# Moving side work between the hooks of a hand-scheduled macaron block: convolution sums one step ahead of their products, moments and the half chunk spread, a few rescales from VectorE to ScalarE

## Chip, cores and metric

The kernel runs on one core of one Trainium2 chip. The metric is device microseconds of one launch, the median of the runs. The profiled execution is a separate launch: it has a time of its own, and a span from its first to its last instruction in the trace.

## What is computed

The input `u` is 2 x 1024 x 1024 in fp32, that is 2048 rows of 1024. Three residual stages follow each other, the first and the third with the same 4-bit weights:

```python
x = x + 0.5 * ffn(layernorm(x))
x = x + s4(layernorm(x))            # long convolution over the last axis
x = x + 0.5 * ffn(layernorm(x))

def ffn(x):                         # W = scales[group] * (w4 - (z4[group] + 1)), groups of 128 rows
    h = silu(x @ Wg) * (x @ Wu)     # Wg, Wu: 1024 x 2752
    return h @ Wd                   # Wd: 2752 x 1024

def s4(u):                          # K: 1024 taps from 64 complex poles
    y = irfft(rfft(u, n=2L) * rfft(K, n=2L), n=2L)[..., :L]
    return y + D[0] * u
```

The kernel computes the convolution as products with 128 x 128 Toeplitz blocks of K, made from Lambda, p, q, Vc, B, Ct and the step size while other work runs.

## The kernel before

**Jobs.** The 2048 rows are cut into four blocks of 512 (`TB`), each held as four tiles of 128 rows. A job is one block in one of the two feed-forward stages; `JOBS` (L756) lists eight: blocks 0 and 1 in stage 1, blocks 0 and 1 in stage 3, then the same for blocks 2 and 3. They are numbered j = 0 to 7. A job is `gate_up` (L766) followed by `down` (L856). The convolution of a block whose stage-1 job was j-1 runs beside the `gate_up` of job j, so in jobs 1, 2, 5 and 6. The tables of K are made once, beside `gate_up` of job 1.

**gate_up.** 64 steps, numbered s: eight waves (`WAVES`) of eight groups g of 128 input rows. The first five waves hold three chunks of 128 output columns each, the last three two; the very last also has the half chunk, which is the 64 columns left over from 2752. A chunk has two units, gate (even number) and up (odd number). A unit owns one of the eight 512-column PSUM banks. In a step each unit gets two products (L795), one with the low part of the normalized input in fp16 and one with the high part in fp32r. The group scale is not put into the weights. After each group except the last the running sum in PSUM is multiplied by a ratio of scales (`scaled`, L758): a rescale, by ScalarE at L760 (called ACT in the profile) or by VectorE at L764 (DVE). Even units go to ACT, odd ones to DVE, and in jobs 0 and 1 the first odd unit of the wave goes to ACT in some steps (L808). After the last group of a wave, `gated` (L820) makes silu of the gate on ACT (L822), multiplies by the up unit on DVE (L825), and splits the result on GpSimd (POOL) into an fp32r high part (L827) and a low part (L829). `gated_half` (L832) does so for the half chunk; its split (L844, L846) is run on DVE at once in job 0, and on POOL at steps 1 and 2 of `down` in the other jobs.

**down.** 44 steps, numbered d: two halves a of the 1024 output columns, each with 22 chunks f. A step has eight products (L870), on four banks c, and then four rescales: banks 0 and 2 on ACT, 1 and 3 on DVE, and in job 0 bank 1 also on ACT at even f (L878). The results go back to rows and into x at hooks of the next job.

**Weights.** Weight bytes are loaded four steps ahead by SyncE (SP, `load_bytes`, L713) and cast three steps ahead by POOL (`make_weights`, L730, the cast at L737), into five buffers.

**Hooks.** All other work is cut into pieces by generators, and `fast` (L1512) hangs each piece on a step of `up` or `dn`; a half step means the middle of the step. Some pieces are wrapped in `in_order_of_writing` (L143) or `pinned`, which adds order dependencies on the named engines only. Otherwise the order on each engine is settled by a scheduler when the program is built, which takes the order of writing as its starting point but need not keep it. The pieces that the change touches:

- moments (`moments_by_tile`, L182: eight bn_stats of 128x512 and four small aggregates, and then `guess`, L196, three tiny instructions), deviations (`deviations_in_pieces`, L213: three Newton steps of three tiny instructions each, and a factor), normalizations (L259, L263), all on DVE. In job 0 they are for block 1 and hang on `down` of job 0. There `turn_by_pool` (L243) follows: four transposes on PE, a copy on ACT, a cast and a subtraction on POOL, for each half tile.
- in `down` of job 1 the normalizations for job 2 (L1646), and `turn_by_dma` (L265), which splits on POOL and transposes by DMA.
- the tables (`s4_tables`, L1207): 63 pieces spread over steps 1 to 42 of `gate_up` of job 1 (L1618). They hold small products on PE (`s4_sums` L1076, `s4_k` L1156, and two of 128x512 from L1185 on), and many small operations on DVE and POOL.
- the convolution (`convolve`, L1219): six block sums in three instructions on POOL (L1227 to L1229), then products in two halves (L1232), then additions into x on DVE. For tile t it hangs on `gate_up` at a base step o: turning from o on, the store at o+4, the load of columns at o+7, sums and the first half of the products at o+10, the second half at o+11 (L1570 to L1577).

Of the kernel before, what the change touches and what calls it, by code (L numbers as in the profile page):

```python
# [32 lines left out]
GK = 8  # L33
# [24 lines left out]
def macaron_s4_kernel(  # L58
# [123 lines left out]
    def moments_by_tile(b, k, halves=False):  # L182
# [11 lines left out]
        guess(b, k, mv)  # L194

    def guess(b, k, mv):  # L196
        name = f"{b}_{k}"
        ve = small.tile([P, NT], F32, tag="ve", name=f"ve_{name}")
        nc.vector.tensor_scalar(ve, mv[:, :, 1], EPS, None, ALU.add)
        r = small.tile([P, NT], F32, tag="r", name=f"r_{name}")  # L200
        half = small.tile([P, NT], I32, tag="half", name=f"half_{name}")
        nc.vector.tensor_scalar(half, ve.bitcast(I32), 1, None, ALU.logical_shift_right)
        nc.vector.tensor_scalar(
            r.bitcast(I32), half, -1.0, float(0x5F3759DF), ALU.mult, ALU.add
        )
        ln[b] = (mv, ve, r)
# [559 lines left out]
    def gate_up(j, b, hooks):  # L766
        hi, lo = pieces[b]
        ps = {}
        for s, (wi, g) in enumerate(STEPS):
# [9 lines left out]

            early = (len(order) + 1) // 2  # L780
            turns = [(k, pos, k == 1) for k in range(2) for pos in range(early)]
            turns += [(k, pos, k == 0) for k in (1, 0) for pos in range(early, len(order))]
            for i, (k, pos, done) in enumerate(turns):
# [21 lines left out]
                if g < GK - 1:  # L805
                    on_act = unit % 2 == 0
                    if unit == 2 * fs[0] + 1:
                        on_act = (j == 0 and g % 4 == 0) or (j == 1 and g % 2 == 0)  # L808
                    if unit == 2 * WIDE:
                        on_act = g % 2 == 0  # L810
# [21 lines left out]
    def gated_half(j, p):  # L832
# [15 lines left out]
        half_split[j] = split(nc.gpsimd if j else nc.vector)  # L848
        if j == 0:
            for _ in half_split[j]:  # L850
                pass

    half_split = {}
    yT = {}

    def down(j, b, hooks):  # L856

        steps = [(a, f) for a in range(NH) for f in range(NF)]
        for d, (a, f) in enumerate(steps):
# [5 lines left out]
            for c in range(4):  # L865
# [12 lines left out]
                on_act = c % 2 == 0 or (j == 0 and c == 1 and f % 2 == 0)  # L878
                if f < GD - 1:
# [179 lines left out]
    def s4_roots():  # L1059
# [13 lines left out]
        for i in range(2):  # L1073
            src = c_eight[i].rearrange("(r v c) -> r v c", r=8, v=8)[:, 0, :]
            nc.sync.dma_start(eight[:, i], src.partition_broadcast(P))
        ps = bank("s4_sums")  # L1076
# [57 lines left out]
    def s4_response():  # L1134
# [20 lines left out]
        yield  # L1155
        ps = bank("s4_k")  # L1156
# [10 lines left out]
    def s4_toeplitz():  # L1167
# [14 lines left out]
        for i in range(NH):  # L1182
            for _ in range(4 - 2 * i):
# [33 lines left out]
    S4_PIECES = 63  # L1217

    def convolve(b, t, s, name):  # L1219
# [9 lines left out]
        nc.gpsimd.tensor_tensor(sums[:, 3], sums[:, 0], sums[:, 1], ALU.add)  # L1229

# [281 lines left out]
    def fast():  # L1512
# [5 lines left out]
        for j, (b, k) in enumerate(JOBS):  # L1518
# [7 lines left out]
            if prev:  # L1526
# [9 lines left out]
                if pk == 1:  # L1536
                    first, start_, gap = (26, 36, 3.5) if j == 1 else (13, 23, 4)
                    steps = [(up, first + (i if j == 1 else (3 * i // 2) / 2)) for i in range(8)]
                    in_pieces(at, steps, lambda: moments_by_tile(pb, 2, halves=True))
                    steps = [(up, start_ + i - 4 if j != 1 else start_ - 2 + i / 2) for i in range(4)]  # L1540
# [29 lines left out]
                    for t in range(NT):  # L1570
# [4 lines left out]
                        at(up, o + 7, pinned(lambda t=t: columns_loaded(t), ET.SP))  # L1575
                        at(up, o + 10, lambda t=t: conv(t))
                        at(up, o + 11, lambda t=t: next(parts[t], None))  # L1577
                    steps = [(up, start_ + gap * t + 13 + i) for t in range(NT) for i in range(2)]
                    in_pieces(at, steps, lambda: moments_by_tile(pb, 3, halves=True))
                    done = start_ + gap * 3 + 15  # L1580
                    steps = [(up, done + i / (2 if j == 1 else 1)) for i in range(4)]
# [32 lines left out]
            if j == 1:  # L1614
                tables = s4_tables()
                for i in range(S4_PIECES):
                    piece = lambda: in_order_of_writing(lambda: next(tables, None), ET.DVE)
                    at(up, 1 + 42 * i // S4_PIECES, piece)  # L1618
            if j == 3:
                in_pieces(at, [(up, 36 + i) for i in range(24)], in_order)  # L1620
            if after:
                ab, ak = after
                if ak == 1:
                    at(up, 55 if j == 0 else 6, lambda: load_x(ab, rows_of(u, ab)))
                    if j == 0:
                        steps = [(dn, d) for d in range(4, 22, 2)]
                        in_pieces(at, steps, lambda: moments_by_tile(ab, 1, halves=True))
                        steps = [(dn, d) for d in (20.5, 21, 21.5, 22)]
                        in_pieces(at, steps, lambda: deviations_in_pieces(ab, 1, LIFT))
                    else:  # L1630
                        steps = [(up, s) for s in range(12, 21)]
# [12 lines left out]
                for t in range(NT):  # L1644
                    for half in range(2):
                        d, where = (23 + 4 * t + 2 * half if j == 0 else (0.5, 6, 14, 20)[t] + half), dn  # L1646
# [5 lines left out]
                    if j == 0:  # L1652
                        for half in range(2):
                            piece = lambda t=t, half=half: turn_by_pool(ab, t, half)
                            at(dn, 25 + 4 * t + 2 * half, piece)
                        continue
                    late = (12, 13) if t == NT - 1 else (13, 17)
                    for d in (1, 2, 3, 5, 6, 7, 9) + late:
                        piece = lambda t=t: turning(t)
                        piece = lambda piece=piece: in_order_of_writing(piece, ET.Pool, ET.SP)  # L1660
                        at(dn, 2 + 9 * t + d, piece)
            for d in (1, 2) if j else ():
# [225 lines left out]
```

## Time and profile before

| what | value |
|---|---|
| runs | 2067.83, 2064.02, 2063.87 us; median 2064.02 |
| the profiled execution, its time | 2064.28 us |
| its span in the trace | 2062.2 us |
| from the start to the first product of job 0 | 22.6 us |
| `gate_up` of job 0 | 178.3 us, PE busy 166.81 |
| `down` of job 7 ends at | 2051.8 us; 10.4 us follow |
| the costliest rescales | L760 on ACT, pg: 1256 of 660 ns; L764 on DVE, pg: 1152 of 691 ns |

A group in the profile is one line of the program, one engine, one operation and one kind of tile, with busy time, mean duration and the idle time ahead of it. The tile names are those of the program: `pg` is a bank of `gate_up`, `po` one of `down`, `pc` and `pb` are the convolution's, `xTh` and `xTl` the two parts of the input, `hh` and `hl` those of the gated product, `hb` the half chunk. The profiler's names for the engines are PE (TensorE), PEld (its weight loads), DVE (VectorE), ACT (ScalarE), POOL (GpSimd) and SP (SyncE). PEclk is the clock that the chip granted to TensorE, as a share of full speed.

### The profile page before, as it was taken

The numbers are of one execution on the slowest core, as the hardware profiler recorded it, in microseconds if no ns is written. First come the engines' busy times: TensorE is split into PE (matmuls) and PEld (weight loads), VectorE is DVE, ScalarE is ACT, GpSimd is POOL, SyncE is SP. The second block draws the span as 40 slices with busy tenths as digits, with TensorE's granted clock in tenths as the row PEclk, the third lists the DMA queues.
The fourth block names the chain that finished last, engine by engine and source line by source line (L and its number), as shares of the span: only waits on it lengthen the run. The fifth ranks groups of instructions, "written<-read, shape, count | busy, mean of one in ns | idle before, by whom it ended". The sixth has DMA issues, their size and how long they took to land.

```text
span 2062.2 us, 29944 instructions
## 1 busy us (share of the span) xinstructions
PE 2011.6 (98%) x9204; PEld 1370.9 (66%) x9204; DVE 1666.7 (81%) x2861; ACT 1397.5 (68%) x2185; POOL 1349.8 (65%) x1740
## 2 busy tenths in 40 slices
PE   6999999999999999999999999999999999999998
PEld 4555675567866778655876568667686576866576
DVE  8888978777888787888778877887878878777777
ACT  6777787756675476767777777664776646767775
POOL 5867668656875478755867568763696645965542
PEclk9999999999999999999999999999999999999999
DMA  4435323233623327511462116333163331661113
GB/s 139 124 90 146 110 83 84 56 83 89 172 78 80 92 50 166 165 32 35 112 176 94 32 46 159 97 77 85 45 156 109 72 92 41 152 186 46 34 35 102
DMA packets 346888, 197.16 MB, mean 96 GB/s; under 512 B 168069, under 2 KB 324590, under 8 KB 346718
## 3 DMA queue, kind: packets, MB, share of 16 engines
q1 hardware_dynamic: 345414, 192.74, 35.0%
q8 instruction: 75, 1.23, 0.3%
q10 hardware_dynamic: 1016, 1.82, 0.2%
q14 instruction: 95, 0.78, 0.1%
q0 software_dynamic: 288, 0.59, 0.1%
HBM read 127.52 MB, written 48.57 MB: 85 GB/s over the span
## 4 chain that ended last, share of the span: by engine, by line
PE 88%; DVE 4%; POOL 2%; DMA 2%; issue 1%; ACT 1%; SPq 0%; ACTq 0%; POOLq 0%; DVEq 0%
PE pg L795 54%; PE po L870 29%; PE pc L1232 3%; PE pb L1232 1%; DVE pg L764 1%; DMA b<-wq 1%; POOL hh L827 0%; DMA bd<-wdq 0%; POOL hl L829 0%; ACT pg L760 0%; POOL w_up L737 0%; POOL q L644 0%; DVE po L764 0%; ACT g L822 0%; DMA x<-in_L_attn_u_dram 0%
## 5 line engine op out<-in xcount | busy, mean ns | idle before, releaser
L760 ACT ACTIVATE pg<-pg,rat 128x512 f32<-128x512 f32 x1256 | 794.0, 660 | 399.5 <-PE pg L795 396.7
L764 DVE TENSOR_TENSOR pg<-pg,rat 128x512 f32<-128x512 f32 x1152 | 764.7, 691 | 144.7 <-PE pg L795 136.9
L795 PE MATMUL pg<-xTh,w_up 128*128 128x512 f32 x2752 | 854.2, 438 | 2.6 <-DVE pg L764 1.3
L795 PE MATMUL pg<-xTl,w_up 128*128 128x512 f16 x2752 | 718.4, 382 | 10.5 <-DVE pg L764 4.3
L737 POOL CAST w_up<-b 128x768 fp32r<-128x768 int8 (+2 forms) x490 | 374.8, 771 | 399.2 <-PE pg L795 289.1
L795 PEld LDWEIGHTS pg<-xTh,w_up 128*128 128x128 f32 x2752 | 519.2, 189 | 171.2 <-issue 10.3
L760 ACT ACTIVATE po<-po,ratd 128x512 f32<-128x512 f32 x660 | 433.4, 662 | 155.5 <-PE po L870 155.1
L870 PE MATMUL po<-hl,w_down 128*128 128x512 f32 x1344 | 526.2, 394 | 5.7 <-DVE po L764 5.4
L870 PE MATMUL po<-hh,w_down 128*128 128x512 f32 x1344 | 520.6, 390 | 0.0
L764 DVE TENSOR_TENSOR po<-po,ratd 128x512 f32<-128x512 f32 x620 | 429.3, 695 | 110.1 <-PE po L870 109.4
L795 PEld LDWEIGHTS <-w_up 128*128 128x128 bf16 x2752 | 226.5, 98 | 350.2 <-issue 168.5
L737 POOL CAST w_down<-bd 128x512 fp32r<-128x512 int8 x352 | 217.6, 621 | 155.1 <-PE po L870 77.9
L870 PEld LDWEIGHTS po<-hl,w_down 128*128 128x128 f32 x1344 | 251.7, 188 | 69.5 <-DVE po L764 11.3
L870 PEld LDWEIGHTS po<-hh,w_down 128*128 128x128 f32 x1344 | 252.4, 188 | 50.9
L829 POOL TENSOR_TENSOR hl<-hf,hh 128x512 fp32r<-128x512 f32 x168 | 218.7, 1302 | 7.0
L827 POOL CAST hh<-hf 128x512 fp32r<-128x512 f32 x168 | 107.5, 640 | 74.5 <-DVE hf L825 44.2
L825 DVE SCALAR_TENSOR_TENSOR hf<-pg,rat,g 128x512 f32<-128x512 f32 x168 | 122.5, 747 | 37.1 <-ACT g L822 28.8
L822 ACT ACTIVATE g<-pg,rat 128x512 f32<-128x512 f32 x168 | 110.1, 686 | 44.5 <-PE pg L795 29.0
L922 POOL TENSOR_TENSOR x<-x,yr 128x512 f32<-128x512 f32 x52 | 66.7, 1283 | 0.0
L289 POOL TENSOR_TENSOR lo<-x,hi 128x512 f16<-128x512 f32 x48 | 61.8, 1288 | 0.0
L189 DVE BATCH_NORM_STATS2 stats<-x 128x6 f32<-128x512 f32 x88 | 59.9, 680 | 0.0
L287 POOL TENSOR_TENSOR mid<-hi,top 128x512 bf16<-128x512 f32 x48 | 56.0, 1166 | 0.0
(216 smaller groups left out, 1080.2 us busy)
## 6 DMA issues: line engine op xcount, KB each, us to landing
b<-wq SPq DMA_DIRECT2D x319, 96.0 KB
bd<-wdq SPq DMA_DIRECT2D x336, 64.0 KB
x<-in_L_attn_u_dram SPq DMA_DIRECT2D x30, 512.0 KB
yz<-y SPq DMA_DIRECT2D x56, 256.0 KB
yr<-yz SPq DMA_DIRECT2D x56, 256.0 KB
b<-wq SPq DMA_DIRECT2D x128, 64.0 KB
sz<-xn SPq DMA_DIRECT2D x16, 512.0 KB
st<-sz SPq DMA_DIRECT2D x64, 128.0 KB
```

The source lines that it names most:

```text
L289: nc.gpsimd.tensor_tensor(lo[:, own], n[:, own], hi[:, own].bitcast(F32), ALU.subtract)
L737: nc.gpsimd.tensor_copy(t, b)
L760: nc.scalar.activation(dst, src, AF.Copy, scale=sc)
L764: nc.vector.tensor_tensor(dst, src, sc.to_broadcast(list(dst.shape)), ALU.mult)
L795: nc.tensor.matmul(p, weights, (lo, hi)[k][:, g, :], start=(g == 0 and not done), stop=(g == GK - 1 and done), skip_group_check=True,)
L822: nc.scalar.activation(g, pg, AF.Silu, scale=rat[:, 2 * f, GK - 1 :])
L825: nc.vector.scalar_tensor_tensor(hf, pu, last, g, ALU.mult, ALU.mult)
L827: nc.gpsimd.tensor_copy(hi, hf)
L829: nc.gpsimd.tensor_tensor(lo, hf, hi.bitcast(F32), ALU.subtract)
L870: nc.tensor.matmul(ps[c], w[:, bass.ts(c, P)], part, start=(f == 0 and k == 0), stop=(f == NF - 1), skip_group_check=True,)
L922: nc.gpsimd.tensor_tensor(part, part, rows_back.pop((a, t)), ALU.add)
L1232: nc.tensor.matmul(dst, lhsT, rhs, start=start, stop=stop, skip_group_check=True)
```

## The change

It has nine edits. No arithmetic is added or removed; work moves in time or between engines.

- `convolve` yields after its three sums. The sums now hang on o+9, the first half of the products on o+10, the second on o+11; the columns are loaded at o+6 instead of o+7.
- `guess` becomes `guess_in_pieces`, its three instructions in three pieces. So the moments have two pieces more, and every list of their steps is lengthened by two (or one).
- In `gate_up`, in the last group of a wave of three chunks, the fourth and fifth unit change places in PE's order.
- In jobs 3 and 4 the first odd unit of a wave is rescaled by ACT in steps 25 to 32.
- The half chunk of job 0 is split on POOL, at steps 12 and 13 of `down`.
- In `down`, bank 1 is rescaled by ACT in seven steps of job 1 and in three steps of job 7.
- The tables get empty pieces: two ahead of `s4_sums`, two more ahead of `s4_k`, two more ahead of the first large product, and none between the first and the second (two fewer). They run as 69 pieces over 43 steps.
- Beside `gate_up` of the convolving jobs, moments and deviations shift by a step or half a step.
- In `down` of job 0 the moments run at steps 4 to 16 in steps of 1.5 instead of 4 to 20, the deviations at 17 to 20 instead of 20.5 to 22, normalizations and transposes one step later. In `down` of job 1 the first normalizations stand at steps 2 and 3 instead of 0.5 and 1.5, and the first tile's turning one step later.

```diff
-        guess(b, k, mv)
+        yield from guess_in_pieces(b, k, mv)
...
+    def guess_in_pieces(b, k, mv):
...
         nc.vector.tensor_scalar(ve, mv[:, :, 1], EPS, None, ALU.add)
+        yield
...
         nc.vector.tensor_scalar(half, ve.bitcast(I32), 1, None, ALU.logical_shift_right)
+        yield
...
+            if n == 3 and g == GK - 1:
+                order[3], order[4] = order[4], order[3]
...
                         on_act = (j == 0 and g % 4 == 0) or (j == 1 and g % 2 == 0)
+                        on_act = on_act or (j in (3, 4) and 24 < s < 33)
...
-        half_split[j] = split(nc.gpsimd if j else nc.vector)
-        if j == 0:
-            for _ in half_split[j]:
-                pass
+        half_split[j] = split(nc.gpsimd)
...
+    relief = {1: (2, 3, 6, 7, 14, 15, 20), len(JOBS) - 1: (36, 38, 40)}
...
                 on_act = c % 2 == 0 or (j == 0 and c == 1 and f % 2 == 0)
+                on_act = on_act or (c == 1 and d in relief.get(j, ()))
...
+        yield
+        yield
         ps = bank("s4_sums")
...
+        yield
+        yield
         yield
         ps = bank("s4_k")
...
-            for _ in range(4 - 2 * i):
+            for _ in range(6 - 4 * i):
                 yield
...
-    S4_PIECES = 63
+    S4_PIECES = 69
...
         nc.gpsimd.tensor_tensor(sums[:, 3], sums[:, 0], sums[:, 1], ALU.add)
+        yield
...
-                    first, start_, gap = (26, 36, 3.5) if j == 1 else (13, 23, 4)
+                    first, start_, gap = (25, 36, 3.5) if j == 1 else (13, 23, 4)
                     steps = [(up, first + (i if j == 1 else (3 * i // 2) / 2)) for i in range(8)]
+                    steps += [(up, first + 7.5 if j == 1 else 18.5), (up, first + 8 if j == 1 else 19)]
...
-                    steps = [(up, start_ + i - 4 if j != 1 else start_ - 2 + i / 2) for i in range(4)]
+                    steps = [(up, start_ + i - 3.5 if j != 1 else start_ - 2 + i / 2) for i in range(4)]
...
-                        at(up, o + 7, pinned(lambda t=t: columns_loaded(t), ET.SP))
-                        at(up, o + 10, lambda t=t: conv(t))
+                        at(up, o + 6, pinned(lambda t=t: columns_loaded(t), ET.SP))
+                        at(up, o + 9, lambda t=t: conv(t))
+                        at(up, o + 10, lambda t=t: next(parts[t]))
                         at(up, o + 11, lambda t=t: next(parts[t], None))
...
+                    steps += [(up, start_ + gap * 3 + 14.5), (up, start_ + gap * 3 + 15)]
...
-                    steps = [(up, done + i / (2 if j == 1 else 1)) for i in range(4)]
+                    steps = [(up, done + 0.5 + i / (2 if j == 1 else 1)) for i in range(4)]
...
-                    at(up, 1 + 42 * i // S4_PIECES, piece)
+                    at(up, 1 + 43 * i // S4_PIECES, piece)
...
-                        steps = [(dn, d) for d in range(4, 22, 2)]
+                        steps = [(dn, 4 + (3 * i) / 2) for i in range(8)] + [(dn, 15.5), (dn, 16)]
...
-                        steps = [(dn, d) for d in (20.5, 21, 21.5, 22)]
+                        steps = [(dn, d) for d in (17, 18, 19, 20)]
...
-                        steps = [(up, s) for s in range(12, 21)]
+                        steps = [(up, s) for s in range(12, 21)] + [(up, 20.5)]
...
-                        d, where = (23 + 4 * t + 2 * half if j == 0 else (0.5, 6, 14, 20)[t] + half), dn
+                        d, where = (24 + 4 * t + 2 * half if j == 0 else (2, 6, 14, 20)[t] + half), dn
...
-                            at(dn, 25 + 4 * t + 2 * half, piece)
+                            at(dn, 26 + 4 * t + 2 * half, piece)
...
-                        at(dn, 2 + 9 * t + d, piece)
-            for d in (1, 2) if j else ():
+                        at(dn, 2 + 9 * t + d + (j == 1 and t == 0), piece)
+            for d in (1, 2) if j else (12, 13):
```

More of the change, by code (lines that the diff above doesn't have):

```diff
@@ L193, in moments_by_tile @@
             yield
-        guess(b, k, mv)
+        yield from guess_in_pieces(b, k, mv)
     def guess(b, k, mv):
+        for _ in guess_in_pieces(b, k, mv):
+            pass
+    def guess_in_pieces(b, k, mv):
         name = f"{b}_{k}"
```

## The prediction

> **What bounds the kernel now.** I read the page's busy shares first.
>
> ```profile
> span 2062.2 us, 29944 instructions
> ...
> PE 2011.6 (98%) x9204; PEld 1370.9 (66%) x9204; DVE 1666.7 (81%) x2861; ACT 1397.5 (68%) x2185; POOL 1349.8 (65%) x1740
> ```
>
> PE, the matrix engine, is busy 98% of the span, and 88% of the chain that ended last is PE at lines 795 and 870. No product is removed, so only PE's waits can be won. Of its 50.6 us of idleness (2062.2 - 2011.6), 14.7 lie before the first product (22.6 us, of which small work on PE fills 7.86) and 8.4 behind the last (10.4, 2.04 filled); the change touches neither. Another 11.5 (178.3 - 166.81) lie in the up stage of job 0, where only the swapped pair acts. So 16.0 us are within reach. The second view is the busy time in the stretches between the first products of the stages: here down of job 0, up and down of jobs 1 and 2, up of jobs 3, 4 and 7, down of job 7.
>
> ```profile
> core 0: us, PE busy (x) PEld busy (x) DVE busy (x) ACT busy (x) POOL busy (x), PEclk, DMA share, GB/s
> 200.90:292.90 92.00, 87.45 (x394) 67.62 (x392) 74.35 (x129) 69.44 (x113) 66.94 (x96) 1.00 0.34 98
> 292.90:483.30 190.40, 187.83 (x905) 118.62 (x905) 146.65 (x295) 128.83 (x209) 120.65 (x182) 1.00 0.32 82
> 483.30:564.20 80.90, 79.73 (x347) 63.90 (x346) 67.44 (x102) 55.45 (x85) 70.05 (x90) 1.00 0.52 131
> 564.20:747.30 183.10, 181.06 (x880) 116.98 (x880) 152.13 (x282) 110.39 (x174) 100.53 (x123) 1.00 0.29 76
> 747.30:825.70 78.40, 78.40 (x346) 64.50 (x344) 61.15 (x94) 55.52 (x85) 68.82 (x90) 1.00 0.59 136
> 825.70:982.20 156.50, 155.62 (x691) 92.93 (x691) 132.63 (x231) 110.45 (x174) 93.23 (x114) 1.00 0.25 75
> 1060.60:1216.50 155.90, 155.21 (x689) 93.31 (x689) 128.73 (x213) 110.48 (x174) 92.17 (x111) 1.00 0.25 74
> 1817.90:1972.80 154.90, 154.90 (x690) 93.33 (x689) 117.90 (x180) 110.54 (x174) 91.53 (x111) 1.00 0.25 76
> 1972.80:2051.80 79.00, 79.00 (x346) 64.16 (x344) 63.27 (x102) 55.63 (x85) 30.52 (x46) 1.00 0.24 70
> ```
>
> The third figure is the length, and stages with the same products can be compared. An undisturbed down stage takes 78.4, an undisturbed up stage without convolution 154.9. Job 0's down is 13.6 above that; its 48 transposes at some 0.11 us each explain 5.3, so 8.3 are waits and the slack around them. Job 1's down is 2.5 above, job 3's up 1.6, job 4's 1.0, job 7's down 0.6. Job 1's up is 7.3 above job 2's, of which its table products (20 small ones at some 0.11, 4 of 128x512 in fp32 at some 0.4) explain 3.8. The clock is 1.00 in all of them. The third view, PE's waits, names the causes.
>
> ```profile
> PE pb L1232 <- POOL sums L1227: 5.7, 6, 1.7
> PE pg L795 <- DVE pg L764: 5.6, 15, 0.8
> PE po L870 <- DVE po L764: 5.4, 7, 1.8
> ```
>
> Asked by stage: the first row is 1.9 in each of jobs 2, 5 and 6, none in job 1. Of the second, 3.5 lie in job 0's up and 0.7 each in jobs 1, 3 and 4. Of the third, 4.3 lie in job 0's down and 1.2 in job 1's. Job 1's up adds 0.9 (tables, POOL), 0.6 (tables, DVE) and 0.4 (tables, a DMA).
>
> **Sums a step ahead.** This is the headline, worth up to 5.7 us of waits and about 0.4 us per job of restarting PE. The wait is made here, in POOL's timeline:
>
> ```profile
> 655.33 0.61 POOL L827 CAST hh<-hf 128x512 fp32r<-128x512 f32 x1
> 655.90 0.99 POOL L1227 TENSOR_TENSOR sums<-st 128x384 f32<-128x384 f32 x1
> 656.84 1.27 POOL L829 TENSOR_TENSOR hl<-hf,hh 128x512 fp32r<-128x512 f32 x1
> ```
>
> PE's product on the sums starts at 656.94, when the first of them is done. But the order in which the engines execute is not the order of the hooks: a scheduler places each instruction. Comparing both built programs engine by engine, POOL's and SP's orders, and the waits on them, are the same from the middle of job 1's down to the end: in job 2 the sums still stand behind the cast of chunk 11 and ahead of its low part. PE's order there differs only in the swapped pair. So I give this edit nothing in jobs 2, 5 and 6 (bounds 0 to 6.9). In job 1 it moves sums of tiles 1 to 3 by one place and loads for tile 2 ahead of one weight load on SP; PE did not wait there, so 0.
>
> **Job 0's down.** Three things change. First, the half chunk leaves DVE for POOL. DVE's rows of it beside POOL's of the other seven jobs:
>
> ```profile
> L844 POOL CAST hb<-hf_half x7: 609/610/687, 489.5 to 1978.6; 64x512 fp32r<-64x512 f32 x7
> L846 POOL TENSOR_TENSOR hb<-hf_half,hb x7: 1285/1288/1291, 490.2 to 1980.0; 64x512 fp32r<-64x512 f32 x7
> L844 DVE CAST hb<-hf_half x1: 424/424/424, 202.3 to 202.3; 64x512 fp32r<-64x512 f32 x1
> L846 DVE TENSOR_TENSOR hb<-hf_half,hb x1: 1582/1582/1582, 203.5 to 203.5; 64x512 fp32r<-64x512 f32 x1
> ```
>
> On DVE it costs 0.42 + 1.58 + 0.06 of gaps = 2.06 us at 202.3 to 205.1, ahead of the first rescale (205.80), for which PE waits until 206.54, then until 209.91 for the next two. On POOL it costs 0.61 + 1.29 = 1.90 around steps 12 and 13, where POOL is busy 5.9 us of 10 (221 to 231) and the chunk isn't used until step 21: hidden. The Trainium skill speaks against such a move: its page "Perfetto Trace Analysis", section "Optimizing Scalar/DVE Operations", warns that the two engines share a port to SBUF, so that offloading from one to the other might not help. By the rule the gain would be near 0. The row for it: in job 3 a normalization took 1.47 instead of 0.53 us at 913.76, while POOL's 1.29 us subtraction (913.66 to 914.95) ran. By the rows, though, that price is paid once, at most 1.3 us, at a step where DVE is not waited for, while the 2.06 go where PE stands still. I take the rows: the second rescale follows its product instead of DVE's queue, 1.8 us (bounds 0.7 to 2.1).
>
> Second, eight moments of about 0.6 us start in steps 4 to 14.5 instead of 4 to 20, and the 14 tiny instructions of guess and deviations (0.5 us each at 243.85 to 246.7, then 0.16) go from steps 20 to 22 into steps 15.5 to 20. Today they hold up the last rescales of the first half, and PE waits 1.8 us until 250.90. Third, normalizations and transposes stand one step later. Summing DVE's durations between successive rescales in the new order gives 32.5 us for 17 steps of 1.83 = 31.1, with a lag of up to 2 us in steps 15 to 20; DVE is busy 9.7 of 10 us at 231 to 241 already. So of 1.8 + 0.2 us waited there now, and 0.3 of restarting, I keep 1.0 as a new wait nearer the middle: 1.3 us won (bounds 0 to 2.6). Together **3.1 us**.
>
> **Job 1's up.** Table pieces run 69 in 43 steps instead of 63 in 42, so each is some 6% earlier until the added empty steps before three products. In the new order DVE's last pole weights stand before the three gated chunks instead of between them, POOL's response sums before cast 35 instead of behind chunk 10, and the two turning products at steps 38 and 39 instead of 36 and 38. The waits 0.6, 0.9 and 0.4 and their restarts (2.3 in all) should go. What becomes late is POOL's building of the tables: 5.9 us that now stand behind chunks 12 to 14. Counted through with POOL's durations, cast 46 ends at 420.7 on the old clock, against step 46 at 421.3: 0.6 us of cover, and where it fails PE waits the difference, up to 1.5 us. ScalarE's copy of the first half (0.7) now stands ahead of three gates. I subtract 0.6 for both: **1.7 us** (bounds 0 to 3).
>
> **Rescales to ScalarE.** Job 1's down, steps 2, 3, 6, 7, 14, 15, 20: exactly where normalizations stand; tile 0's move to 2 and 3. PE's 1.2 us of waits with restarts are 1.7, and 0.8 more is slow pitch around them; ScalarE then has three rescales of 0.60 (start to start when queued) in a step of 1.83 us, which fits. I take **1.5** (0.8 to 2.4). Jobs 3 and 4, steps 25 to 32: the wait at step 33 (0.49 and 0.47, with restart 0.65 and 0.63) is on the rescale that moves; the one at step 25 (0.22 each) is on step 24's, which does not. ScalarE gets four rescales, 2.4 of 2.69 us; job 1's up has the same four in every second step and no wait of PE on ScalarE. **1.4** (0.8 to 2.4). Job 7's down: three steps, no wait there: 0.1 (-0.3 to 0.4).
>
> **The swapped pair** in the last step of a wave: one chunk's gate is ready 0.22 us earlier, another's product 0.22 later. DVE waits 0.13 us for that gate; PE does not wait in jobs 5 to 7. It costs nothing where the next wave has two free banks to cover it: 0 (-0.5 to 0.5 over all jobs).
>
> **Sum:** 3.1 + 1.7 + 1.5 + 1.4 + 0.1 = 7.8. The profiled execution took 2064.28 around its span of 2062.2, the median of the runs is 2064.02, so they may be equated: 2056.2.
>
> **Rivals.** (a) As worked out, 0.60: 2056.2, own range 2053.5 to 2059.5. (b) Waits only move: DVE is full in job 0's down and POOL in job 1's up, only jobs 1, 3 and 4's rescales and 1 us of the half chunk are won: 3.9, so 2060.1; 0.22. For it speaks DVE's 9.7 of 10 us. (c) The sums do come earlier after all: 6.9 more, 2049.3; 0.06; against it, the identical order. (d) Everything in job 0's down goes, and both bounds of job 1: 12 us, 2052; 0.08. (e) Slower: ScalarE with four of six rescales delivers each step late. Over 7 + 7 + 7 + 3 = 24 relieved steps a lateness of 0.7 us each costs 16.8 against the other 4.8 gained: 2076; it decides from 0.37 us a step (8.9 us: the 4.8, and the 4.1 that count as slower). Four spaced at 0.60 leave 0.29 us of a step, so it needs rescales slower than any row here; 0.04.
>
> **Numbers.** About 0.2%, 4.1 us, is what a measurement of this kernel can tell from no change: faster means under 2059.9. Case (a) nearly whole, half of (b), (c) and (d): 0.84; the rest of (b) and a little of (a): 0.12; (e): 0.04. The range runs from (d) to past (b): 2052.0 to 2061.0, leaving out (c), (e) and tails.
>
> **What would show it.** Down of job 0 near 89, its waits on rescales under 2 us and none near step 23; up of job 1 near 188.7; down of job 1 near 79.4; jobs 3 and 4 near 155.5 and 155.3; up of jobs 2, 5 and 6 still 183.1 with 1.9 of waits on the sums each. Wrong would be: those three shorter, a wait of PE on ScalarE in jobs 3 and 4, or on weights around step 46 of job 1.

## The result, and the profile after

The changed kernel takes 2054.72 us (median; 2053.31 to 2055.47) against 2064.02 (2063.34 to 2067.83): a ratio of 0.9949, 95% interval 0.9934 to 0.9963. Forecast were 2056.2 and a range of 2052.0 to 2061.0. The profiled execution took 2054.89 us, against 2064.28 before. These are the head of its page, and the stretches of the same nine stages, in the same columns as before (length third, then busy time of PE, PEld, DVE, ACT and POOL, then the clock):

```profile
span 2053.0 us, 29946 instructions
...
PE 2007.7 (98%) x9204; PEld 1371.8 (67%) x9204; DVE 1653.2 (81%) x2836; ACT 1409.5 (69%) x2208; POOL 1353.4 (66%) x1742
```

```profile
199.30:289.10 89.80, 87.54 (x394) 67.55 (x392) 73.64 (x127) 69.50 (x113) 68.60 (x98) 1.00 0.34 100
289.10:477.80 188.70, 186.77 (x906) 119.39 (x905) 149.62 (x294) 128.99 (x209) 120.32 (x182) 1.00 0.32 83
477.80:556.80 79.00, 78.77 (x347) 64.45 (x346) 63.81 (x97) 58.54 (x91) 69.80 (x90) 1.00 0.54 134
556.80:739.90 183.10, 181.04 (x881) 116.97 (x881) 152.12 (x282) 110.49 (x174) 100.93 (x123) 1.00 0.29 76
739.90:818.30 78.40, 78.40 (x347) 64.50 (x346) 61.21 (x94) 55.54 (x85) 69.01 (x90) 1.00 0.58 135
818.30:974.20 155.90, 155.50 (x692) 92.96 (x691) 128.32 (x224) 114.01 (x181) 93.43 (x114) 1.00 0.25 76
1052.60:1207.70 155.10, 154.88 (x690) 93.23 (x689) 124.41 (x206) 113.96 (x181) 92.28 (x111) 1.00 0.25 75
1808.70:1963.30 154.60, 154.60 (x688) 93.12 (x687) 117.68 (x179) 110.56 (x173) 91.98 (x111) 1.00 0.25 76
1963.30:2042.00 78.70, 78.70 (x347) 64.47 (x346) 61.18 (x99) 57.05 (x89) 30.45 (x46) 1.00 0.24 70
```

Row by row, beside the table of before: down of job 0 is 2.1 us shorter, up and down of job 1 are 1.8 and 1.9 shorter, job 2 has not moved, jobs 3 and 4 are 0.6 and 0.8 shorter, the two stages of job 7 0.3 each. PE's waits tell the same. In this view each row gives the total in us, the number and the longest:

```profile
PE pg L803 <- DVE pg L770: 5.8, 15, 1.0
PE pb L1245 <- POOL sums L1239: 5.8, 6, 1.7
...
PE po L877 <- DVE po L770: 1.3, 2, 1.1
PE po L877 <- DVE e L224: 0.7, 1, 0.7
```

The wait on the sums, which the headline of the change is about, is untouched (5.7 before). The wait of `down` on DVE fell from 5.4 to 1.3, but 0.7 came up beside it, with a tiny instruction of the deviations named as its releaser. The wait of `gate_up` on DVE is the same in sum (5.6 before) and not in place. POOL's timeline shows that the sums have not moved at all: cast of the last chunk, sums, low part, as before.

```profile
647.92 0.61 POOL L836 CAST hh<-hf 128x512 fp32r<-128x512 f32 x1
648.49 0.99 POOL L1239 TENSOR_TENSOR sums<-st 128x384 f32<-128x384 f32 x1
649.43 1.27 POOL L838 TENSOR_TENSOR hl<-hf,hh 128x512 fp32r<-128x512 f32 x1
```

### The profile page after: what moved, and what is told of

It reads as the page before. It is cut to its first block, busy times and chain, and to the rows that moved or that the text cites. A ratio compares the mean times of both kernels' runs of the same rounds, so it can differ in the third digit from the quotient of the medians.

```text
span 2053.0 us, 29946 instructions
## 1 busy us (share of the span) xinstructions
PE 2007.7 (98%) x9204; PEld 1371.8 (67%) x9204; DVE 1653.2 (81%) x2836; ACT 1409.5 (69%) x2208; POOL 1353.4 (66%) x1742
## 4 chain that ended last, share of the span: by engine, by line
PE 91%; DVE 3%; POOL 2%; DMA 1%; issue 1%; ACT 1%; SPq 0%; ACTq 0%; POOLq 0%; DVEq 0%
PE pg L803 56%; PE po L877 30%; PE pc L1245 3%; PE pb L1245 1%; DVE pg L770 1%; DMA b<-wq 1%; POOL hh L836 0%; POOL w_up L743 0%; ACT pg L766 0%; POOL hl L838 0%; DMA x<-in_L_attn_u_dram 0%; POOL q L650 0%; POOL sums L1239 0%; DMA st<-sz 0%; DVE hf L834 0%
## 5 line engine op out<-in xcount | busy, mean ns | idle before, releaser
L770 DVE TENSOR_TENSOR pg<-pg,rat 128x512 f32<-128x512 f32 x1138 | 755.1, 692 | 142.9 <-PE pg L803 135.2
L766 ACT ACTIVATE po<-po,ratd 128x512 f32<-128x512 f32 x669 | 438.0, 662 | 144.0 <-PE po L877 143.1
L770 DVE TENSOR_TENSOR po<-po,ratd 128x512 f32<-128x512 f32 x611 | 423.8, 696 | 112.0 <-PE po L877 111.3
```

The costliest lines, as they stand in the source:

```text
L766: nc.scalar.activation(dst, src, AF.Copy, scale=sc)
L770: nc.vector.tensor_tensor(dst, src, sc.to_broadcast(list(dst.shape)), ALU.mult)
```

## The experiments

All stage lengths below, in us, are distances between the first products of successive stages in the trace of one execution; where the clock stays at 1.00 they repeat within some 0.3 us from trace to trace, and within 0.5 in down of job 0 of kernels that have the same order there. Medians and intervals come from the timed runs; a ratio compares the runs of both kernels and need not be the quotient of the medians shown. The kernel before was timed again with each group: its median was 2064.74 beside half, mom, relief and tab, 2064.72 beside conv, swap, dev and pin2, and 2065.28 beside shift, pin, best and dve.

| kernel | median | ratio, interval | job 0 down | job 1 up | job 1 down | job 2 up | job 3 up | job 4 up |
|---|---|---|---|---|---|---|---|---|
| before | 2064.02 | | 91.97 | 190.40 | 80.87 | 183.15 | 156.49 | 155.92 |
| after | 2054.72 | 0.9949, 0.9934 to 0.9963 | 89.84 | 188.63 | 79.00 | 183.14 | 155.88 | 155.12 |
| half | 2064.13 | 0.9999, 0.9990 to 1.0008 | 90.05 | 191.42 | 81.08 | 183.19 | 156.51 | 155.85 |
| mom | 2064.57 | 1.0003, 0.9994 to 1.0012 | 92.06 | 191.96 | 81.18 | 183.11 | 156.50 | 155.98 |
| relief | 2060.93 | 0.9988, 0.9980 to 0.9997 | 92.07 | 191.84 | 78.58 | 183.15 | 155.96 | 155.31 |
| tab | 2062.63 | 0.9991, 0.9982 to 1.0000 | 93.67 | 188.92 | 80.87 | 183.15 | 156.61 | 156.09 |
| conv | 2065.10 | 1.0002, 0.9993 to 1.0011 | 91.93 | 192.26 | 80.86 | 183.10 | 156.53 | 156.00 |
| swap | 2064.33 | 0.9999, 0.9991 to 1.0008 | 93.75 | 191.90 | 80.92 | 183.12 | 156.65 | 155.93 |
| shift | 2065.69 | 1.0000, 0.9991 to 1.0008 | 93.83 | 192.28 | 79.94 | 183.13 | 156.65 | 155.94 |
| dev | 2055.92 | 0.9958, 0.9943 to 0.9974 | 89.63 | 188.50 | 79.00 | 183.17 | 156.01 | 155.21 |
| pin | 2052.93 | 0.9940, 0.9924 to 0.9955 | 89.75 | 188.52 | 79.02 | 182.08 | 156.09 | 155.21 |
| pin2 | 2048.59 | 0.9924, 0.9911 to 0.9938 | 89.37 | 188.51 | 79.00 | 180.77 | 156.01 | 155.24 |
| best | 2048.20 | 0.9917, 0.9904 to 0.9931 | 89.82 | 188.49 | 78.99 | 180.73 | 155.49 | 154.91 |
| dve | 2045.45 | 0.9904, 0.9889 to 0.9920 | 88.87 | 188.51 | 79.03 | 180.76 | 155.62 | 154.75 |

**half**, the kernel before with the half chunk of job 0 on POOL:

```diff
-        half_split[j] = split(nc.gpsimd if j else nc.vector)
-        if j == 0:
-            for _ in half_split[j]:
-                pass
+        half_split[j] = split(nc.gpsimd)
...
-            for d in (1, 2) if j else ():
+            for d in (1, 2) if j else (12, 13):
```

> The kernel before with one edit: the half chunk of job 0 is split on POOL at steps 12 and 13 of down instead of on DVE at once. Theory A (the whole gain of job 0's down comes from here; the spread moments give nothing): down of job 0 shortens by 2.2 us, from 91.97 to 89.8, with the waits of steps 2 and 3 shorter and the 1.8 us wait at step 23 still there. Theory B (the prediction: 1.8 from here and 1.3 from the moments): 90.2. If sharing with DVE ate the gain, as the rule weighed in the prediction has it: 91.5 or more. Total: 2061.8 by A, 2062.2 by B.

**mom**, the kernel before with the moments part alone (`guess` in three pieces belongs to it; the diff begins behind that):

```diff
...
-                        steps = [(dn, d) for d in range(4, 22, 2)]
+                        steps = [(dn, 4 + (3 * i) / 2) for i in range(8)] + [(dn, 15.5), (dn, 16)]
...
-                        steps = [(dn, d) for d in (20.5, 21, 21.5, 22)]
+                        steps = [(dn, d) for d in (17, 18, 19, 20)]
...
-                        d, where = (23 + 4 * t + 2 * half if j == 0 else (0.5, 6, 14, 20)[t] + half), dn
+                        d, where = (24 + 4 * t + 2 * half if j == 0 else (0.5, 6, 14, 20)[t] + half), dn
...
-                            at(dn, 25 + 4 * t + 2 * half, piece)
+                            at(dn, 26 + 4 * t + 2 * half, piece)
```

> The kernel before with one edit: moments and deviations for block 1 spread earlier in down of job 0 (with the guess in three pieces), normalizations and transposes there one step later; the half chunk stays on DVE. Theory A (the wait only moves): the wait at step 23 (1.8) goes, but waits and slow steps between 15 and 20 take its place, and down of job 0 stays within 0.3 us of 91.97. Theory B (the prediction): 1.3 us won, 90.7.

The half chunk alone shortens down of job 0 by 1.92 us, the moments alone by nothing (longer by 0.09). The timed runs of half can't show its gain (0.9999; 1.92 us would be 0.9991, inside the interval); it rests on the stage lengths. PE's waits in that stage, first of half, then of mom:

```profile
PE po L867 <- DVE po L764: 3.4, 3, 1.8
```

```profile
PE po L876 <- DVE po L770: 2.3, 2, 1.4
PE po L876 <- ACT po L766: 0.7, 2, 0.4
PE po L876 <- DVE e L224: 0.7, 1, 0.7
```

In half the 1.8 us wait at step 23 is still there, and the stage is shorter all the same. In mom that wait is gone, and the last two rows hold what stands in its place: 0.4 at step 16 (one of the two waits on ACT; the other, of 0.3, is that of step 2, which before had too), and 0.7 at step 19 for a rescale behind the deviations. Steps 16 and 19 take 2.5 and 2.9 us in mom, 2.0 and 1.8 before; step 23 takes 1.8, before 3.9. Over steps 4 to 20, into which the moments and deviations were moved, first of before, then of mom, in the columns of the stretches:

```profile
212.20:244.90 32.70, 32.53 (x138) 24.63 (x138) 29.49 (x53) 25.20 (x40) 23.53 (x39) 1.00 0.39 112
```

```profile
211.80:246.70 34.90, 33.85 (x138) 23.84 (x138) 31.53 (x64) 25.09 (x40) 23.59 (x39) 1.00 0.42 121
```

DVE has 2.0 us more to do there (the third busy figure), and the steps are 2.2 us longer: what step 23 gave back, they took. The moved work costs PE as much where it is now as where it was. Between the two theories half alone doesn't decide (90.05 lies between 89.8 and 90.2, nearer to the prediction's figure); mom does, with 92.06 where the prediction's theory wanted 90.7. The other reading in the expectation of half, that the shared port eats the gain, falls: it would have needed 91.5 or more, 90.05 was measured, and the rows of the half chunk in the changed kernel (job 0's now among the eight) have nearly the median durations of before:

```profile
L853 POOL CAST hb<-hf_half x8: 607/610/687, 224.9 to 1969.4; 64x512 fp32r<-64x512 f32 x8
L855 POOL TENSOR_TENSOR hb<-hf_half,hb x8: 1277/1286/1345, 226.2 to 1970.8; 64x512 fp32r<-64x512 f32 x8
```

**dev**, the changed kernel with the deviations in ten pieces:

```diff
             nc.vector.tensor_tensor(e, r, r, ALU.mult)
+            if single:
+                yield
             nc.vector.tensor_tensor(e, e, ve, ALU.mult)
+            if single:
+                yield
...
-                        steps = [(dn, d) for d in (17, 18, 19, 20)]
+                        steps = [(dn, 16.5 + i / 2) for i in range(10)]
```

> The changed kernel with one edit: the deviations for block 1 in down of job 0 as ten pieces, half a step apart from step 16.5, most of them one tiny instruction. Theory: in the changed kernel four of these tiny instructions follow each other at 237.9 to 240.1, each on the result of the one before, and take 0.54 us each instead of some 0.15 between rescales; PE waits 0.7 us for the rescale behind them. Spread, the wait goes and down of job 0 falls from 89.84 to 89.0 (0.9 won). Rival (DVE is simply full from step 15 to 20, and the order of the tiny ones does not matter): within 0.2 of 89.84.

My theory fell. The wait of 0.7 behind the deviations went, but 0.26 came back at step 23, and the stage takes 89.63, inside the 89.37 to 89.84 of the four kernels that have the change's own order there (after, pin, pin2, best). How the tiny instructions are grouped is not what limits.

Nor does a tiny instruction take 0.5 us because it reads the result of the one ahead of it, as that expectation has it. In the kernel before, the same two lines follow each other twice, and POOL is at work until 246.72 and then idle until 247.81:

```profile
245.66 0.51 DVE L218 TENSOR_TENSOR e<-r 128x4 f32<-128x4 f32 x1
246.21 0.52 DVE L219 TENSOR_TENSOR e<-e,ve 128x4 f32<-128x4 f32 x1
247.18 0.15 DVE L218 TENSOR_TENSOR e<-r 128x4 f32<-128x4 f32 x1
247.37 0.17 DVE L219 TENSOR_TENSOR e<-e,ve 128x4 f32<-128x4 f32 x1
```

```profile
244.43 1.17 POOL L673 COPY qd<-rawd 128x512 int8<-128x512 int8 x2
245.55 1.17 POOL L737 CAST w_down<-bd 128x512 fp32r<-128x512 int8 x2
247.81 0.62 POOL L737 CAST w_down<-bd 128x512 fp32r<-128x512 int8 x1 [1.09 <-PE po L870]
```

The fourteen traces hold 2198 instructions of DVE with an output of 128x4. The 296 that took 0.3 us or more all had POOL at work for over 90% of their time, and none of the 1332 that ran with POOL idle took more than 0.173; 312 stayed short although POOL was at work. In down of job 0 the long ones cost DVE 1.8 to 2.7 us beyond 0.165 each, about as much as the wait at step 23. So work on POOL does go with slower work on DVE, though the half chunk's own move paid. No run takes POOL's work away from these instructions: the cause, and what it would win, are not shown.

The rival of dev, that DVE is full, was tested by itself in **dve**, which is the kernel best (below) with three rescales more on ACT:

```diff
-    relief = {1: (1, 2, 3, 6, 7, 14, 15, 20), len(JOBS) - 1: (36, 38, 40)}
+    relief = {0: (15, 17, 19), 1: (1, 2, 3, 6, 7, 14, 15, 20), len(JOBS) - 1: (36, 38, 40)}
```

> The next kernel (best) with one edit more: in down of job 0 bank 1 is rescaled by ACT also at steps 15, 17 and 19, so by ACT in every step from 14 to 20. Theory (DVE is full there, which is why the spread moments gave nothing): each step loses 0.6 us of DVE work, the waits of 0.4 and 0.7 at steps 16 and 19 go, and down of job 0 falls from 89.5 to 88.5. Rival (ACT, with three rescales of 0.60 in a step of 1.83, then sets the pace): within 0.3 of 89.5, or longer, with waits on ACT.

Down of job 0 fell by 0.95 (89.82 to 88.87; 1.0 was expected), and it is 0.50 below pin2, the shortest with the change's own order there. Steps 15 to 20, first of best, then of dve, in the columns of the stretches:

```profile
230.60:244.10 13.50, 12.35 (x50) 8.35 (x49) 12.98 (x29) 7.93 (x13) 9.55 (x16) 1.00 0.56 166
```

```profile
229.30:241.90 12.60, 12.40 (x50) 8.50 (x50) 12.03 (x27) 9.55 (x16) 10.28 (x17) 1.00 0.49 146
```

DVE's busy time (the third busy figure) goes from 12.98 to 12.03, and the stretch is shorter by 0.90, while PE's own work is the same. ACT took 9.55 of 12.60 and was not in the way. So DVE's work over these steps was the limit (12.98 of 13.50 in best), and spreading work inside them (dev) did not win anything.

**conv**, the kernel before with the headline edit alone:

```diff
+        yield
...
-                        at(up, o + 7, pinned(lambda t=t: columns_loaded(t), ET.SP))
-                        at(up, o + 10, lambda t=t: conv(t))
+                        at(up, o + 6, pinned(lambda t=t: columns_loaded(t), ET.SP))
+                        at(up, o + 9, lambda t=t: conv(t))
+                        at(up, o + 10, lambda t=t: next(parts[t]))
```

> The kernel before with one edit, the headline: convolve yields after its sums, the sums hang on o+9, the products on o+10 and o+11, the columns are loaded at o+6. Theory A (the scheduler orders POOL by itself, and its order is the same from job 2 on): jobs 2, 5 and 6 keep 183.1 us and 1.9 us of waits on the sums each; nothing won there, within 0.1 us each. Rival (the hook does act): waits of under 0.5 and 180.8 us each. In job 1 the products on tile 2 stand earlier in PE's order; that may move its up stage by 0.5 us either way.

Up of jobs 2, 5 and 6 took 183.10, 183.07 and 183.13, with 2.1 us of waits in each, 1.9 of it on the sums. The edit wins nothing. Was the wait worth anything, then? **pin** hangs the sums of tiles 0 and 2 a further step earlier in jobs 2, 5 and 6 and fixes their place on POOL against what was written before them; **pin2** also fixes the cast of the finished wave's first chunk behind them. Both are the changed kernel with

```diff
-                        at(up, o + 9, lambda t=t: conv(t))
+                        early = j != 1 and t % 2 == 0
+                        at(up, o + 9 - early, pinned(lambda t=t: conv(t), ET.Pool))
```

and pin2 has in `gated` besides

```diff
-        nc.gpsimd.tensor_copy(hi, hf)
+        high_part = lambda: nc.gpsimd.tensor_copy(hi, hf)
+        if j in (2, 5, 6) and f in (9, 12):
+            in_order_of_writing(high_part, ET.Pool)
+        else:
+            high_part()
```

> The changed kernel with only the first half of the step that moved the sums: they are hung one step earlier with their place in POOL's order fixed against what was written before, and nothing is fixed behind them. POOL's order then has the sums of tile 0 ahead of the last chunk's high part (0.6 us) instead of behind it, and those of tile 2 ahead of one low part and one more cast. If POOL's queue sets the wait, it shrinks by what stands ahead of the sums no more: tile 0 from 1.69 to 1.1, tile 2 from 0.24 to 0; up of jobs 2, 5 and 6 at 182.2 each. If something else set it (the arrival of the columns, or the place of the products), the waits stay at 1.9.

> The changed kernel with one edit: in jobs 2, 5 and 6 the sums of tiles 0 and 2 are hung one step earlier still, at o+8, with their place in POOL's order fixed, and the high part of the first chunk of the finished wave fixed behind them. Theory (the sums are late because they stand behind casts and low parts of the finished wave in POOL's queue, not because their columns are late): PE's waits on the sums (1.9 us in each of the three jobs) go, with 0.4 of restart; up of jobs 2, 5 and 6 from 183.1 to 180.9 each, 2054.7 to 2048.1. Rival 1 (the columns have not landed at step 31): POOL waits for a DMA ahead of the gated chunks, and the stages are 183 or longer. Rival 2 (the delayed gated chunks hold up the next weights or the banks): the waits on the sums go, but waits on weights or on gates come, and less than half is won.

The wait shrinks with what stands ahead of the sums in POOL's queue: in pin, with one cast less ahead of the sums of tile 0, it is 1.1 us for these and none for tile 2, and the stage takes 182.1 instead of 183.1; in pin2 it is gone, and the stage takes 180.7. POOL's timeline in pin2, and its up stages of jobs 2, 5 and 6:

```profile
643.40 0.83 POOL L743 CAST w_up<-b 128x768 fp32r<-128x768 int8 x1 [1.88 <-PE pg L803]
644.20 1.01 POOL L1243 TENSOR_TENSOR sums<-st 128x384 f32<-128x384 f32 x1
645.17 0.72 POOL L1244 TENSOR_TENSOR sums<-st 128x256 f32<-128x256 f32 x1
645.86 0.45 POOL L1245 TENSOR_TENSOR sums<-sums 128x128 f32<-128x128 f32 x1
646.25 0.60 POOL L836 CAST hh<-hf 128x512 fp32r<-128x512 f32 x1
```

```profile
556.70:737.40 180.70, 180.55 (x881) 116.80 (x881) 151.94 (x282) 110.37 (x174) 100.36 (x123) 1.00 0.30 77
1283.90:1464.50 180.60, 180.45 (x881) 116.84 (x881) 151.89 (x282) 110.38 (x174) 100.37 (x123) 1.00 0.30 77
1542.90:1723.60 180.70, 180.55 (x882) 116.93 (x881) 152.01 (x282) 110.56 (x174) 100.37 (x123) 1.00 0.29 77
```

PE idles 0.15 us in each instead of 2.1. The three stages are 7.3 us shorter than before in sum (549.38 to 542.07), a little more than the bound of 6.9 that the prediction gave; the median is 6.1 below the changed kernel's (2048.59 against 2054.72). Both rivals of pin2 fall: the columns were there, and no wait on weights came.

**relief** is the kernel before with the three parts that give rescales to ACT and the later start in down of job 1; **shift** has only the latter:

```diff
-                        d, where = (23 + 4 * t + 2 * half if j == 0 else (0.5, 6, 14, 20)[t] + half), dn
+                        d, where = (23 + 4 * t + 2 * half if j == 0 else (2, 6, 14, 20)[t] + half), dn
...
-                        at(dn, 2 + 9 * t + d, piece)
+                        at(dn, 2 + 9 * t + d + (j == 1 and t == 0), piece)
```

> The kernel before with one edit: the rescales given to ACT (down of jobs 1 and 7, up of jobs 3 and 4), and the first normalizations in down of job 1 moved to steps 2 and 3. Both theories of the result say that this part is independent of the others: down of job 1 from 80.87 to 79.0, up of jobs 3 and 4 from 156.49 and 155.92 to 155.9 and 155.1, down of job 7 from 79.05 to 78.8; 3.6 us in all, so about 2060.4. If part of it needed the swapped pair or the earlier tables, job 1's down or job 3's up would stay longer than that by 0.5 or more. The rival that ACT falls behind would show as new waits of PE on ACT.

> The kernel before with one edit: the first normalizations of down of job 1 at steps 2 and 3 instead of 0.5 and 1.5, and the first tile's turning one step later; no rescale goes to ACT. Down of job 1 was 80.87 before and 78.58 with shift and relief together. If the relief does the work, as the prediction has it: 80.3 or more. If the shift does it: under 79.5.

Down of job 1 is 78.58 with relief and shift and 79.94 with the shift alone: 0.9 from the shift, 1.4 from the rescales. Neither side of the expectation of shift holds; the two share the gain. Jobs 3 and 4 gave 0.53 and 0.61. Down of job 7 gave nothing: 79.11, where 78.8 was expected and 79.05 measured before. The kernels with the whole change have 78.78 to 78.98 there, so something shortens it by some 0.2, but the rescales alone don't. PE waits nowhere on ACT in down of job 1. In the changed kernel that stage is 0.4 longer than in relief: PE waits 0.23 at step 1. There the last step of the deviations, moved half a step later by the change, stands between the half chunk's gate and the last two gates on DVE (0.39 us in pin2, 0.16 and earlier in relief). That this is the cause is read from the order, not tested.

**tab**, the kernel before with the tables' empty pieces:

```diff
+        yield
+        yield
         ps = bank("s4_sums")
...
+        yield
+        yield
         ps = bank("s4_k")
...
-            for _ in range(4 - 2 * i):
+            for _ in range(6 - 4 * i):
...
-    S4_PIECES = 63
+    S4_PIECES = 69
...
-                    at(up, 1 + 42 * i // S4_PIECES, piece)
+                    at(up, 1 + 43 * i // S4_PIECES, piece)
```

> The kernel before with one edit: the tables' empty pieces and 69 pieces over 43 steps. Theory A (the gain of job 1's up comes from the tables alone): up of job 1 from 190.40 to 188.6, with no wait of PE on the three table products. Rival (it comes partly from the moments, the sums and the loads that also moved there): only the waits of 0.6, 0.9 and 0.4 go, but new waits on rescales appear where table pieces now stand ahead of them, and the stage ends between 188.9 and 190.4.

Up of job 1 is 188.92; the gain comes from the tables, with 0.3 to 0.4 from the other moves. But the rival has a part of it right: the three waits on the tables (1.8 in sum) are gone, and the waits on DVE's rescales rise from 0.7 to 1.8, one of 1.0 at step 21:

```profile
PE pg L795 <- DVE pg L764: 1.8, 4, 1.0
```

**swap**, the kernel before with the swapped pair:

```diff
+            if n == 3 and g == GK - 1:
+                order[3], order[4] = order[4], order[3]
```

> The kernel before with one edit: the fourth and fifth unit swapped in the last group of a wave of three chunks. After the change the up stage of job 0 was 1.5 us shorter (178.35 to 176.84) and that of job 7 0.3, though only this edit reaches them. Theory A (the swap does it): 176.9 and 154.6 here, some 2 us in all. Rival (job 0's up varies between executions, by when its first loads land): job 0's up in this run and in the other runs of kernels with the old order lies anywhere between 176.8 and 178.4, and only job 7's 0.3 is the swap's.

Up of job 7 took 154.89 (154.90 before), up of job 0 178.19 (178.35 before). In all fourteen traces up of job 0 lies between 176.0 and 179.4, whichever order it has. The 1.5 us that the changed kernel's trace shows there are scatter of that stage, not the change.

**best** is pin2 with

```diff
-    relief = {1: (2, 3, 6, 7, 14, 15, 20), len(JOBS) - 1: (36, 38, 40)}
+    relief = {1: (1, 2, 3, 6, 7, 14, 15, 20), len(JOBS) - 1: (36, 38, 40)}
...
-                        on_act = on_act or (j in (3, 4) and 24 < s < 33)
+                        on_act = on_act or (j in (3, 4) and 23 < s < 33)
```

> The kernel with the sums fixed on POOL and two more rescales given to ACT: bank 1 at step 1 of down of job 1, and step 24 in the up stages of jobs 3 and 4, where PE still waits 0.23 on DVE. Theory: down of job 1 from 79.0 to 78.6, up of jobs 3 and 4 from 156.0 and 155.2 to 155.6 and 154.8; 1.2 us in all, 2048.6 to 2047.4. Rival (ACT has the gate at step 24 as well and is late with the even units): no gain there, or a wait of PE on ACT.

Against pin2, jobs 3 and 4 gave 0.52 and 0.33; down of job 1 did not move (78.6 was expected), so the wait at its step 1 is not on the rescale that I moved. In the timed runs the difference to pin2 is within scatter. The kernel dve, with this and the relief of job 0, is the fastest: 2045.45 us.

## Why the prediction was right

The sum of the forecast was 7.8 us. The same terms measure 7.5 in the two traces; the rest of the 9.2 us between the spans is mainly up of job 0 (1.5), which is scatter.

- **Sums a step ahead: 0 forecast, 0 measured.** The argument from the order of the built programs held, and conv confirms it. The hook says when a piece is written; the scheduler says where it stands.
- **Half chunk: 1.8 forecast, 1.9 measured** (half). The rows, not the rule about the shared port, gave the right number for this move; that POOL's work goes with slower tiny instructions on DVE (under dev) was not seen then.
- **Moments: 1.3 forecast, nothing measured alone** (mom), 0.2 to 0.7 on top of half. This is the term that was mis-sized. The step said that of 2.3 us "I keep 1.0 as a new wait nearer the middle". Waits of 1.1 came there in place of 0.2, and with longer steps without a listed wait steps 4 to 20 took back 2.2 (32.70 to 34.90), all that step 23 had given. The sum in that same paragraph, 32.5 us of DVE work for 31.1 us of steps, already said that DVE had no room; I took 1.0 off, where all of it was due. (The tiny instructions are thirteen, not fourteen; nothing hangs on it.) The stage came out at 89.84 against "near 89". Rival (b), that waits only move in job 0's down, was right for the moments and wrong for job 1.
- **Job 1's up: 1.7 forecast, 1.8 measured, by other terms.** The table waits went as said. The subtraction was put on the weight cast before step 46 and on the gates behind ScalarE's copy; neither waited. The new wait is on a rescale at step 21, which no step of the prediction named. Waits account for 0.6 of the gain (2.57 to 1.93); the other 1.1 lies in shorter distances from the start of one product to the next, 0.6 among the job's own and 0.5 among those of the tables and the convolution.
- **Rescales to ScalarE: 1.5, 1.4 and 0.1 forecast, 1.9, 1.4 and 0.3 measured.** Of the 1.9 the later start of the normalizations alone gives 0.9 (shift), and the 0.3 in job 7 is not shown to come from its rescales (relief). The 0.22 at step 25 stayed, as said, and went when its own rescale was moved (best). Rival (e), ScalarE late, didn't come: no relieved step of any kernel has a wait of PE on ScalarE, with up to three rescales of 0.60 in a step of 1.83, or four in 2.69.
- **Swapped pair: 0 forecast, 0 measured.**

So the total was right partly by luck: the moments gave some 1 us less than forecast, the stages with rescales 0.6 more. And the medians differ by 9.3, of which these terms make 7.5. Most of the rest was not in the forecast at all and fits the clock drops of the last section. Each timed run has its span and its mean clock on record; the span times what the clock lacks of 1.00 averages 5.7 us in 81 runs of the kernel before and 4.1 in the 27 runs of the six kernels with the whole change. From this the share of the drops can be estimated at 1.6 us. (One reading of the page was wrong and without effect: the 88% of the chain are PE as a whole; lines 795 and 870 have 83%.)

## What to carry to other kernels

Before a wait is priced as won, ask how full the engine is that will do the moved work: where its sum nearly fills a stretch, moving work inside it wins nothing, and only taking work off it does (0.95 us from three rescales, against nothing from the moments and thirteen tiny instructions spread out). A piece that is hooked earlier has moved only if the built order says so; here the hook won 0, and the same sums, hung a step earlier still with their place fixed on their engine and the next user fixed behind them, won 7.3. Test parts by stage lengths in the trace: most single parts here were under what timed runs can tell, and clear in the stage.

## What was not expected of the hardware

A short wait of PE can be followed by a loss as large as itself or larger, and one profile need not show it. In swap, at the 1.8 us wait of step 23 in job 0's down, the granted clock (the third figure from the right) falls to 0.50 for some 3.4 us:

```profile
248.00:250.00 2.00, 0.99 (x5) 0.43 (x3) 2.00 (x7) 1.43 (x3) 0.30 (x1) 1.00 0.95 324
250.00:252.00 2.00, 1.17 (x3) 0.98 (x4) 2.00 (x6) 0.00 (x0) 0.61 (x1) 0.75 0.42 136
252.00:254.00 2.00, 2.00 (x6) 1.51 (x6) 1.36 (x3) 0.99 (x2) 0.61 (x1) 0.50 0.27 69
254.00:256.00 2.00, 2.00 (x12) 1.53 (x11) 0.87 (x2) 1.53 (x4) 0.62 (x1) 0.89 0.27 65
```

and in relief right behind the sixteen tiny table products in job 1's up, which had waited 0.6:

```profile
358.00:360.00 2.00, 2.00 (x17) 1.67 (x17) 0.90 (x3) 0.00 (x0) 2.00 (x4) 0.98 0.23 56
360.00:362.00 2.00, 2.00 (x6) 1.33 (x4) 0.00 (x0) 1.76 (x3) 2.00 (x5) 0.50 0.01 2
362.00:364.00 2.00, 2.00 (x8) 0.85 (x7) 1.11 (x2) 0.71 (x2) 2.00 (x6) 0.66 0.00 0
```

By the clock each costs 1.7 us, half of 3.4; the stages with it are 1.0 to 1.9 us longer. The first place has the drop in 3 of the 7 traces that still have that wait, and in none of the 7 without it; the second in 6 of the 7 with the old table order (191.4 to 192.3 us for the stage), and in none of the 7 with the new (188.5 to 188.9). Of the kernels that have both the wait and the old tables, only the trace of before, from which the forecast was made, has neither drop. So the change is worth more than that trace could tell: an estimate from these counts is 0.7 us in job 0's down (3/7 of 1.7) and 1.5 in job 1's up (6/7 of 1.7), where the mean clocks above give 1.6 for both. The Trainium skill, page "TensorE: Matmul & The Clock Gate", section "HAM oscillation — how this bites in real kernels", has as its rule that PE must not idle for more than about 3.4 us; here drops follow waits of 1.8 and 0.6 us, and the waits of 1.7 us on the sums are followed by none in any of the traces. In job 0's up, where only the swapped pair differs, PE waits 2.8 to 3.7 us for ScalarE at step 16 in every trace. Ten of the fourteen have a drop there, and the four without waited 2.75, 2.87, 3.46 and 3.59 us. So the length of the wait alone doesn't decide; what does stays open.
